# Layer 1's expert pages: answers written over their rows, a fourth single page in flight, and page work placed inside the last steps of the fused pass

## The chip, the cores and the metric

One core of a Trainium2 chip runs the whole program. The metric is the device time of one execution in microseconds (us). Before the change it is 1968.87 us, the median of three runs (1968.59 to 1971.76).

The engines named below are TensorE (PE in the profile, with PEld for its weight loads), VectorE (DVE), ScalarE (ACT), GpSimd (POOL) and SyncE (SP, whose DMA queue is SPq). Each works through its own instructions in order.

## The reference, cut to what matters

The model has two layers. Each is a graph step followed by a mixture of experts. The change touches the end of layer 1's graph step and its mixture:

```python
# x: 128 graphs of 64 nodes, 256 wide = 8192 rows
h = layer_norm(x, ln_gamma, ln_beta)                       # layer 1, graph step
agg = einsum('bij,bjh->bih', adj, h)
conv = einsum('bkh,ho->bko', agg, W_rel) + b_rel + einsum('bkh,ho->bko', h, W_root)
x = x + relu(conv)

xf = layernorm(x).reshape(-1, 256)                         # layer 1, experts
topk_vals, topk_idx = top_k(xf @ Wg + bg + bias, 2)        # 2 of 8 experts for a row
combine = (one_hot(topk_idx, 8) * softmax(topk_vals)[..., None]).sum(axis=1)
h = relu(einsum('td,edh->teh', xf, W1) + b1)               # 256 -> 512
y = einsum('teh,ehd->ted', h, W2) + b2                     # 512 -> 256
x = x + einsum('ted,te->td', y, combine)
```

## The kernel before

**The fused pass.** The pass that ends layer 0 and does layer 1's graph step works through 32 blocks (NB) of 256 rows. Every block goes through a list of stages, each with a lag. The helper `staggered` walks through steps; in step s a stage of lag L works on block s - L, in the order of the list. That order is the order of the instructions on TensorE, VectorE and ScalarE, since these three are scheduled by hand. So the last blocks end in steps 31 to 35, in which more and more stages have no block left.

The stages that matter here, by their functions: `output` (the chain A: residual, statistics, `hn` and `s`), `flip_h` (transposes `hn` on TensorE; ScalarE scales it to `hT`), `neighbours` (products `pz`, copied to `z`), `convolve_a` and `convolve_b` (products `pc`), `residual` (the chain R: x3, its store to the output, `xs`), `flip3` and `gate1` (transposes of `xs`, gate products `pg`), `choice` (the chain H: top two experts, marks `r1hot`), `count1` (counting products `pos`), `slots` (the chain S: the row of each token in its expert's list, `r1row`), and `place1` and `send1`, which send the rows (`xs`) to their experts' lists in a table in HBM (`r1x`) with indirect DMAs from GpSimd, four for a block.

**Pages.** An expert's list is worked off in pages of 256 rows, each with the expert's weights `pw` (W1 and b1) and the bias row `pb2`. W2 stays resident in `fw2`. A page goes through: fetch (`fetch1` asks for the rows `px` and, through `load1`, for `pw` and `pb2`, all from SyncE's queue), `flip1` (transposes to `pxT`), `up` (products `ph`, Relu on ScalarE into `phid`), `down` (products `py`), `share` (the weight p of each row, from the difference of two logits that a row carries in its last column), and `answer`. `answer` adds the bias to `py` into a tile `py_s` (three buffers), multiplies both halves by p, and adds each half to the output with an accumulating indirect DMA from GpSimd (L436), which reads `py_s` and, for the row numbers, column 256 of `px`. The adds of one page wait for those of the page before.

**The first four pages.** The pages numbered -4 to -1 belong to experts 0 to 3. They are known to be full well before the pass ends, so they need not wait for the last rows to be routed. Pages -4, -3 and -2 borrow PSUM banks of the fused pass (`places_of`: the pools `ps`, `po`, and `pz` or `pc` for the answers) and are put into its last steps by `ahead`; an entry (n, f) of `ahead`, in a stage of lag 4, runs f in step 36 + n, so that n = -4 is step 32. Page -1 and all later ones run in the loop after the pass, in which page i is fetched two positions ahead. There the pools `pt`, `ph` and `py` lie over the old banks. `px`, `pw` and `pb2` have three buffers each; `px4`, which holds the rows of a double page (two pages of one expert), has three as well.

**After the pass**, `page_lists` on VectorE (some sixty small instructions on 8 to 32 elements a partition) turns the counts into the lists of double pages, single pages and half pages (`r1tab`). SyncE reads each page's row and expert from it. The profiled execution has 28 double pages.

**Before, in the last steps:** page -4 is transposed in step 31, its up-products are done in two halves in step 32, its down-products in two halves in step 33; page -3 is transposed in step 33, and its up-products are in step 34; pages -3 and -2 are finished after the pass. Page -1's fetch is asked for after the pass, in the order W1, bias row, rows.

Of the kernel before, what the change touches and what calls it, by code (L numbers as in the profile page):

```python
# [9 lines left out]
F32 = mybir.dt.float32  # L10
# [96 lines left out]
class Router:  # L107
# [442 lines left out]
    def page_lists(self, scratch):  # L550

        v, E, n, pg = self.nc.vector, self.E, self.name, self.pg
        used = [0]

        def small(*shape):
            size = shape[0] * shape[-1] if len(shape) > 1 else shape[0]
            used[0] += size
            t = scratch[:, used[0] - size:used[0]]
            return t.rearrange("p (a b) -> p a b", b=shape[1]) if len(shape) > 1 else t

        wide = lambda t, k: t.unsqueeze(k).to_broadcast([P, 4, E])
# [12 lines left out]
        v.tensor_scalar(two, two, MAGIC, None, op0=ALU.add)  # L574
        v.tensor_scalar(two, two, -MAGIC, None, op0=ALU.add)
        v.tensor_scalar(big, left, pg / 2.0, None, op0=ALU.is_gt)
        v.scalar_tensor_tensor(half, left, 0.0, big, op0=ALU.is_gt, op1=ALU.subtract)
        v.scalar_tensor_tensor(one, two, -2.0, full, op0=ALU.mult, op1=ALU.add)
        v.tensor_add(one, one, big)
        le, at = small(4, E), small(4, E)  # L580
        exp, nth, no = (small(4) for _ in range(3))
        most = small(1)
        for m, (num, step) in enumerate(((two, 2 * pg), (one, pg), (half, 0))):
            cum = small(E)
            if m == 0:
                v.scalar_tensor_tensor(row, self.taken, float(pg), self.base, op0=ALU.mult, op1=ALU.add)
            elif m == 1:
                v.scalar_tensor_tensor(row, two, 2.0 * pg, row, op0=ALU.mult, op1=ALU.add)
            else:
                v.tensor_sub(row, self.last, left)  # L590
            v.tensor_tensor_scan(cum, num, self.zero[:, :E], 0.0, op0=ALU.add, op1=ALU.add)
            v.tensor_tensor(le, wide(cum, 1), wide(self.page, 2), op=ALU.is_le)  # L592
            v.tensor_reduce(exp, le, op=ALU.add, axis=AX.X)  # L593
            v.tensor_tensor(at, wide(self.expert, 1), wide(exp, 2), op=ALU.is_equal)  # L594
            v.tensor_mul(at, at, wide(row, 1))  # L595
            v.tensor_reduce(no, at, op=ALU.add, axis=AX.X)
            if step:
# [13 lines left out]
        v.tensor_copy(self.total_pages, most)  # L611
# [55 lines left out]
def two_layer_gnn_moe_kernel(ctx: ExitStack, tc: tile.TileContext, a: dict, out: bass.AP):  # L667
    nc = tc.nc
    x_in, adjT = a["x"], a["adjT"]
    N, D = x_in.shape  # L670
# [83 lines left out]
    W = D + 2  # L754
# [482 lines left out]
    def load1(i, e):  # L1237
        Q = pages[i]
        Q["w"] = w = wx.tile([P, F1W], F32, name="pw", bufs=3)
        nc.sync.dma_start(out=w, in_=fw1[ds(e, 1)].rearrange("o p f -> p (o f)"))  # L1240
        Q["b2"] = b2 = wx.tile([P, D], F32, name="pb2", bufs=3)
        nc.sync.dma_start(out=b2, in_=a["L1_ffn_b2"][ds(e, 1), :].to_broadcast([P, D]))

    def fetch1(i):
# [5 lines left out]
        if what == 0:  # L1250
            Q["x4"] = wx.tile([P, 4, W], F32, name="px4", bufs=3)
            Q["x"] = Q["x4"][:, :2, :]
        else:
            Q["x"] = wx.tile([P, 2, W], F32, name="px", bufs=3)
        if i < 0:
            if i == -FIRST:
                regs["first"] = r1.load_first(0, ENG.SP)
# [17 lines left out]
        Q["xT"] = xT = wx.tile([P, KD, PG], F32, name="pxT")  # L1275
        nc.scalar.copy(xT[:, :, :n * P], pt[:, :, :n * P])

    def up(i, lo=0, hi=KF):
        Q = pages[i]
        w, m = Q["w"], Q["n"] * P  # L1280
        if lo == 0:
            Q["hid"] = wx.tile([P, KF, PG], F32, name="phid")
        hid = Q["hid"]
        for c0 in range(lo, hi, Q["group"]):
            group = range(c0, c0 + Q["group"])
            ph = [Q["ph"](c) for c in group]
            for c in group:
                for k in range(KD):
                    nc.tensor.matmul(ph[c - c0][:, :m], lhsT=w[:, k * F1 + c * P:k * F1 + (c + 1) * P],  # L1289
                                     rhs=Q["xT"][:, k, :m], start=(k == 0), stop=(k == KD - 1))  # L1290
            for c in group:
                nc.scalar.activation(hid[:, c, :m], ph[c - c0][:, :m], AF.Relu,  # L1292
                                     bias=w[:, KD * F1 + c:KD * F1 + c + 1], scale=1.0)

    def down(i, e, tiles=(0, 1)):
        Q = pages[i]
# [17 lines left out]
        nc.vector.tensor_scalar(p, p, 1.0, None, op0=ALU.add)  # L1314
        nc.vector.reciprocal(p, p)

    def answer(i):
        Q = pages[i]
        y, p, n = wx.tile([P, 2, D], F32, name="py_s", bufs=3), Q["p"], Q["n"]
        nc.vector.tensor_add(y[:, :n, :], Q["py"][:, :n, :], Q["b2"].unsqueeze(1).to_broadcast([P, n, D]))  # L1320
        for t in range(n):
            nc.vector.tensor_scalar(y[:, t, :], y[:, t, :], p[:, t:t + 1], None, op0=ALU.mult)  # L1322
            r1.add(i // 2 * 2 if 0 <= i < 2 * ND else i, Q["x"][:, t, :], y[:, t, :])

    with tc.tile_pool(name="c3", bufs=1, reuse_waits="tile") as c3, \
            tc.tile_pool(name="work3", bufs=2, reuse_waits="tile") as work, \
# [238 lines left out]

        for i in (-4, -3, -2):
            places_of(i)

        staggered(NB, (
            (-2, load3),  # L1570
            (-3, load_weights),
            (-4, load_y),
            (2, R),
            (0, A),
            (2, R),
# [14 lines left out]
            (2, R),  # L1590
            (0, A),
            (-2, mixture),
            (1, flip_h),
            (4, ahead((-4, lambda: up(-4, 0, 2)))),
            (2, R),
            (-1, out_proj),
            (3, H),
# [17 lines left out]
            (4, lambda b: send1(b, 3) if b < NB - 2 else None),  # L1615
            (1, convolve_a),
            (3, count1),
            (4, ahead((-3, lambda: down(-4, 0, (0,))), (-2, lambda: up(-3)))),
            (-3, fold),
            (0, A),  # L1620
            (3, S),
# [2 lines left out]
            (0, A),  # L1624
            (3, S),
            (2, flip3),
            (4, ahead((-5, lambda: flip1(-4)), (-3, lambda: flip1(-3)))),
            (1, convolve_b),
            (2, gate1),
            (4, ahead((-8, lambda: fetch1(-4)), (-7, lambda: fetch1(-3)), (-6, lambda: fetch1(-2)),  # L1630
                      (-4, lambda: up(-4, 2)), (-3, lambda: down(-4, 0, (1,))))),
            (0, A),
            (3, S),
            (3, S),
            (3, S),
            (3, place1),
            (4, load_w2),
        ))
        r1.page_lists(work.tile([P, 512], F32, name="scratch", bufs=1))
        share(-4)  # L1640
        answer(-4)
        flip1(-2)
        down(-3, 1)
        up(-2)
        share(-3)
        answer(-3)


    with tc.tile_pool(name="pt4", bufs=2, space=PSUM, reuse_waits="tile") as pt_pool, \
# [7 lines left out]
        def finish(i):  # L1657
            if i >= 0:
                what, m, new = listed(i)
                if i < E1:  # L1660
                    r1.fill_end(i)
                if new and not (what == 0 and i % 2):
                    regs["e", what] = r1.load(what + 1, m, ENG.PE)
            share(i)
            down(i, regs["e", what][m % 4] if i >= 0 else i + FIRST)
            answer(i)

        def then(f):
            return lambda i: f(i) if i > -2 else None

        def fetch(i):
            places_in(i)
            if i > -2:
                fetch1(i)

        def run(order):
# [47 lines left out]
```

## Time and profile before

| | |
|---|---|
| median of three runs | 1968.87 us |
| the profiled execution | 1970.99 us |
| its span, first to last instruction | 1969.2 us |
| TensorE busy | 1852.8 us (94%) |
| VectorE busy | 1146.4 us (58%) |
| ScalarE busy | 1002.0 us (51%) |
| GpSimd busy | 1134.5 us (58%) |
| mean granted TensorE clock | 0.973 |
| fused pass ends, page loop begins | about 1475 us |
| last instruction | about 1958 us |

The profile is of one execution. A page of it sums busy time by engine and by group of instructions; the chain of waits is followed back from the last instruction, at each step to what released it. The timeline lists instructions in order of time: start, duration, engine, line, operation, output and inputs, and in brackets how long the engine stood idle before it and what ended that. In the table of windows each row has, for a stretch of time, the busy time and number of instructions of TensorE, its weight loads, VectorE, ScalarE and GpSimd, then PEclk (the granted TensorE clock as a share of full speed), the share of the DMA engines in use, and GB/s. A line of waits gives who waited for whom, the total in us, how often, and the longest.

### The profile page before, as it was taken

Reading aid. Unit: us, or ns where it says so; the run is one execution under the profiler, and the core shown is the slowest. Engines: PE = TensorE matmul, PEld = TensorE weight load, DVE = VectorE, ACT = ScalarE, POOL = GpSimd, SP = SyncE. Lnnn points to the kernel's source line nnn. Section 1 sums busy time; section 2 is a strip of 40 time slices with the busy share of each in tenths; the row PEclk is TensorE's granted clock in tenths of the full one; section 3 lists DMA queues with packets and bytes.
Section 4 is the critical chain, followed back from the end, with each engine's and each line's share of the span. In section 5 each row is a group of like instructions: output and inputs, shape, how many; then the busy total and the mean of one; then the engine's idle time right before and its main releaser. Section 6 shows DMA issues by size and latency. Waiting matters only on the chain. (4 is left out here: it accounts for less than half of the span.)

```text
span 1969.2 us, 35306 instructions
## 1 busy us (share of the span) xinstructions
PE 1852.8 (94%) x9906; PEld 1613.4 (82%) x9906; DVE 1146.4 (58%) x4256; ACT 1002.0 (51%) x2047; POOL 1134.5 (58%) x1114
## 2 busy tenths in 40 slices
PE   7999999999966899999999899999987999999996
PEld 6888888888845777888877788888876888888885
DVE  5899999999975333344433379999962222222221
ACT  5888888988841222222222266666642333333332
POOL 1377777777677677777777724444443444434443
PEclk9999999999967999999999899999988999999998
DMA  5134555553376988766666799778425666666653
GB/s 139 63 131 143 164 162 163 159 165 131 118 258 216 301 257 264 213 213 206 207 208 191 295 307 337 272 258 281 155 88 129 161 133 130 131 134 130 129 108 48
DMA packets 253085, 359.49 MB, mean 183 GB/s; under 512 B 53176, under 2 KB 210504, under 8 KB 252880
## 3 DMA queue, kind: packets, MB, share of 16 engines
q1 hardware_dynamic: 175904, 210.74, 36.0%
q0 software_dynamic: 62736, 135.21, 23.2%
q10 hardware_dynamic: 14240, 11.12, 1.8%
q8 instruction: 90, 1.47, 0.3%
q14 instruction: 115, 0.94, 0.2%
HBM read 193.27 MB, written 166.03 MB: 182 GB/s over the span
## 5 line engine op out<-in xcount | busy, mean ns | idle before, releaser
L419 POOL DMA_INDIRECT r0x<-xs,r0row x384 | 388.0, 1010 | 216.2 <-ACT lat L883 113.6
L426 POOL DMA_INDIRECT r0y<-px x390 | 378.7, 971 | 122.9 <-DMA r0y<-px 52.2
L1188 PE MATMUL py<-lat,pxT 128*128 x1616 | 385.6, 383 | 21.0 <-ACT pxT L1162 17.7
L436 POOL DMA_INDIRECT out_x<-py_s,px x131 | 202.8, 1548 | 282.5 <-DVE py_s L1322 179.3
L1192 DVE TENSOR_SCALAR px<-py,px 128x256 f32<-128x256 f32 x390 | 171.0, 480 | 306.9 <-PE py L1188 300.7
L1188 PEld LDWEIGHTS py<-lat,pxT 128*128 128x128 f32 x1616 | 293.1, 191 | 60.3 <-ACT pxT L1162 22.2
L1162 ACT COPY pxT<-pt 128x512 f32<-128x512 f32 x188 | 109.7, 586 | 345.3 <-PE pt L1159 241.0
L1292 ACT ACTIVATE phid<-ph,pw 128x256 f32<-128x256 f32 (+1 forms) x264 | 122.0, 462 | 293.0 <-PE ph L1289 180.4
L419 POOL DMA_INDIRECT r1x<-xs,r1row x128 | 134.9, 1054 | 184.1 <-ACT hn L1432 53.9
L894 PE MATMUL ps<-lat 128*128 128x256 f32 x1024 | 240.0, 383 | 0.0
L858 PE MATMUL ph<-lat 128*128 128x256 f32 x1024 | 233.3, 387 | 2.7 <-DVE lat L881 2.0
L1303 PE MATMUL py<-fw,phid 128*128 (+1 forms) x1016 | 232.7, 382 | 0.0
L1289 PE MATMUL ph<-pxT,pw 128*128 128x256 f32 (+1 forms) x1056 | 227.0, 368 | 0.0
L858 PEld LDWEIGHTS ph<-lat 128*128 128x128 f32 x1024 | 195.9, 194 | 29.8 <-issue 2.4
L894 PEld LDWEIGHTS ps<-lat 128*128 128x128 f32 x1024 | 194.3, 192 | 28.3
L1289 PEld LDWEIGHTS ph<-pxT,pw 128*128 128x128 f32 x1056 | 193.0, 190 | 24.7
L1303 PEld LDWEIGHTS py<-fw,phid 128*128 128x128 f32 x1016 | 189.6, 192 | 23.5
L1314 DVE TENSOR_SCALAR p<-p 128x2 f32<-128x2 f32 (+1 forms) x69 | 12.2, 177 | 218.5 <-ACT p L1313 218.5
L1159 PE MATMUL pt<-ident,px 128*128 128x128 f32 x780 | 120.7, 276 | 11.6 <-DMA px<-r0x 11.6
L1320 DVE TENSOR_TENSOR py_s<-py,pb 128x512 f32<-128x512 f32 (+1 forms) x67 | 44.5, 664 | 143.7 <-PE py L1303 141.4
L1159 PEld LDWEIGHTS pt<-ident,px 128*128 128x128 f32 x780 | 97.3, 142 | 36.1 <-issue 10.9
L881 DVE SCALAR_TENSOR_TENSOR lat<-ph,c_L_gnn_b,rms 128x256 f32<-128x256 f32 x256 | 111.9, 476 | 23.0 <-ACT rms L72 22.9
(337 smaller groups left out, 2966.9 us busy)
## 6 DMA issues: line engine op xcount, KB each, us to landing
y<-r0y SPq DMA_DIRECT2D x64, 768.0 KB
px<-r0x SPq DMA_DIRECT2D x376, 129.0 KB
pw<-in_L_ffn_W1b SPq DMA_DIRECT2D x41, 514.0 KB
x<-x SPq DMA_DIRECT2D x64, 256.0 KB
px<-r1x SPq DMA_DIRECT2D x28, 516.0 KB
r0x<-r0filler ACTq DMA_DIRECT2D x64, 129.0 KB
lat<-in_x SPq DMA_DIRECT2D x32, 256.0 KB
lat<-in_L_ffn_lattice_weights SPq DMA_DIRECT2D x8, 1024.0 KB
```

Source lines behind the costliest of these rows:

```text
L419: i = self.nc.gpsimd.indirect_dma_start(out=self.table[:, :], out_offset=bass.IndirectOffsetOnAxis(ap=row[:, t, k:k + 1], axis=0), in_=xs[ ...
L426: d = self.nc.gpsimd.indirect_dma_start(out=self.answer[:, :], out_offset=bass.IndirectOffsetOnAxis(ap=x[:, self.D:self.D + 1].bitcast(I32 ...
L436: i, d = f"{self.name}add{i}", self.nc.gpsimd.indirect_dma_start(out=self.total[:, :], out_offset=bass.IndirectOffsetOnAxis(ap=x[:, self.D ...
L858: nc.tensor.matmul(ph[:, c, :], lhsT=w1[:, k, ts(2 * j + c, P)], rhs=B["aggT"][:, k, :], start=(k == 0), stop=(k == KD - 1))
L881: nc.vector.scalar_tensor_tensor(hT[:, c, :], B["ph", c // 2][:, c % 2, :], b1[:, c:c + 1], B["rms"], op0=ALU.add, op1=ALU.mult)
L894: nc.tensor.matmul(B["po"][:, t, :], lhsT=B["hT"][:, c, ts(t, P)], rhs=w2[:, c, :], start=False, stop=(t == T - 1 and c == KH - 1))
L1159: nc.tensor.transpose(pt[:, k, ts(q, P)], Q["px"][:, q, ts(k, P)], ident)
L1188: nc.tensor.matmul(py[:, q, :], lhsT=xT[q][:, k, ts(h, P)] if parts == 2 else xT[:, k, ts(q, P)], rhs=lat[:, ds(e, 1), k, :].rearrange("p ...
L1192: nc.vector.tensor_scalar(px[:, q, :D], py[:, q, :], px[:, q, D + 1:D + 2], None, op0=ALU.mult)
L1289: nc.tensor.matmul(ph[c - c0][:, :m], lhsT=w[:, k * F1 + c * P:k * F1 + (c + 1) * P], rhs=Q["xT"][:, k, :m], start=(k == 0), stop=(k == KD ...
L1292: nc.scalar.activation(hid[:, c, :m], ph[c - c0][:, :m], AF.Relu, bias=w[:, KD * F1 + c:KD * F1 + c + 1], scale=1.0)
L1303: nc.tensor.matmul(py[:, t, :], lhsT=Q["hid"][:, c, ts(t, P)], rhs=fw2[:, ds(e, 1), c, :].rearrange("p o d -> p (o d)"), start=(c == 0), s ...
```

## The change

It has four parts.

- `answer` is split into `gather` (the bias add), `weight` (the two multiplications) and `add1` (the two adds). The result is written into the first 256 columns of the page's own rows, and `py_s` is gone.
- `px` and `pb2` have four buffers in place of three. Page -1 is fetched in step 32 of the list (its rows and bias row are requested as early as SyncE's queue allows; its weights take page -4's buffer), and not in the loop.
- `up` is split into `products` (TensorE) and `bend` (the Relus on ScalarE), for two of the four column groups at a time, and these are spread over steps 31 to 33. The transposes of pages -4, -3 and -2 move to steps 30, 31 and 33; page -4's down-products, both halves, come between the gate products of step 32 and the counts of step 33; page -4's bias add is at the end of step 33. After the pass page -2's up-products come first, and then page -3's down-products.
- For blocks 30 and 31 `flip_h` stands at the head of the step, and not in its middle. In `page_lists` four small instructions that the list of double pages doesn't need are moved behind that list.

```diff
@@ page_lists
-        v.tensor_scalar(big, left, pg / 2.0, None, op0=ALU.is_gt)
-        v.scalar_tensor_tensor(half, left, 0.0, big, op0=ALU.is_gt, op1=ALU.subtract)
-        v.scalar_tensor_tensor(one, two, -2.0, full, op0=ALU.mult, op1=ALU.add)
-        v.tensor_add(one, one, big)
...
             elif m == 1:
+                v.tensor_scalar(big, left, pg / 2.0, None, op0=ALU.is_gt)
+                v.scalar_tensor_tensor(half, left, 0.0, big, op0=ALU.is_gt, op1=ALU.subtract)
+                v.scalar_tensor_tensor(one, two, -2.0, full, op0=ALU.mult, op1=ALU.add)
+                v.tensor_add(one, one, big)
@@ load1, fetch1
-        Q["b2"] = b2 = wx.tile([P, D], F32, name="pb2", bufs=3)
+        Q["b2"] = b2 = wx.tile([P, D], F32, name="pb2", bufs=4)
...
-            Q["x"] = wx.tile([P, 2, W], F32, name="px", bufs=3)
+            Q["x"] = wx.tile([P, 2, W], F32, name="px", bufs=4)
@@ up becomes products and bend
+    def products(i, c0):
+        Q = pages[i]
+        m = Q["n"] * P
+        for c in range(c0, c0 + Q["group"]):
+            Q["up", c] = Q["ph"](c)
+        for c in range(c0, c0 + Q["group"]):
+            for k in range(KD):
+                nc.tensor.matmul(Q["up", c][:, :m], lhsT=Q["w"][:, k * F1 + c * P:k * F1 + (c + 1) * P],
+                                 rhs=Q["xT"][:, k, :m], start=(k == 0), stop=(k == KD - 1))
+
+    def bend(i, c0):
...
+        for c in range(c0, c0 + Q["group"]):
+            nc.scalar.activation(Q["hid"][:, c, :m], Q["up", c][:, :m], AF.Relu,
+                                 bias=Q["w"][:, KD * F1 + c:KD * F1 + c + 1], scale=1.0)
+
+    def up(i):
+        for c in range(0, KF, pages[i]["group"]):
+            products(i, c)
+            bend(i, c)
@@ answer becomes gather, weight and add1
-        y, p, n = wx.tile([P, 2, D], F32, name="py_s", bufs=3), Q["p"], Q["n"]
-        nc.vector.tensor_add(y[:, :n, :], Q["py"][:, :n, :], Q["b2"].unsqueeze(1).to_broadcast([P, n, D]))
-        for t in range(n):
-            nc.vector.tensor_scalar(y[:, t, :], y[:, t, :], p[:, t:t + 1], None, op0=ALU.mult)
-            r1.add(i // 2 * 2 if 0 <= i < 2 * ND else i, Q["x"][:, t, :], y[:, t, :])
+        y, n = Q["x"], Q["n"]
+        nc.vector.tensor_add(y[:, :n, :D], Q["py"][:, :n, :], Q["b2"].unsqueeze(1).to_broadcast([P, n, D]))
...
+            nc.vector.tensor_scalar(y[:, t, :D], y[:, t, :D], p[:, t:t + 1], None, op0=ALU.mult)
...
+            r1.add(i // 2 * 2 if 0 <= i < 2 * ND else i, Q["x"][:, t, :], Q["x"][:, t, :D])
@@ the list of stages
+        usual = NB - 2
...
+            (1, lambda b: flip_h(b) if b >= usual else None),
             (2, R),
...
-            (1, flip_h),
-            (4, ahead((-4, lambda: up(-4, 0, 2)))),
+            (1, lambda b: flip_h(b) if b < usual else None),
+            (4, ahead((-5, lambda: products(-4, 0)), (-5, lambda: bend(-4, 0)),
+                      (-4, lambda: bend(-4, 2)), (-4, lambda: products(-3, 0)), (-3, lambda: down(-4, 0, (1,))))),
...
-            (4, ahead((-3, lambda: down(-4, 0, (0,))), (-2, lambda: up(-3)))),
+            (4, ahead((-4, lambda: bend(-3, 0)))),
...
-            (4, ahead((-5, lambda: flip1(-4)), (-3, lambda: flip1(-3)))),
+            (4, ahead((-6, lambda: flip1(-4)), (-5, lambda: flip1(-3)), (-3, lambda: flip1(-2)))),
             (1, convolve_b),
             (2, gate1),
             (4, ahead((-8, lambda: fetch1(-4)), (-7, lambda: fetch1(-3)), (-6, lambda: fetch1(-2)),
-                      (-4, lambda: up(-4, 2)), (-3, lambda: down(-4, 0, (1,))))),
+                      (-4, lambda: fetch1(-1)), (-5, lambda: products(-4, 2)), (-4, lambda: down(-4, 0, (0,))),
+                      (-3, lambda: products(-3, 2)))),
...
             (3, place1),
             (4, load_w2),
+            (4, ahead((-3, lambda: bend(-3, 2)), (-3, lambda: gather(-4)))),
         ))
         r1.page_lists(work.tile([P, 512], F32, name="scratch", bufs=1))
-        share(-4)
-        answer(-4)
-        flip1(-2)
+        up(-2)
         down(-3, 1)
-        up(-2)
-        share(-3)
-        answer(-3)
+        for i in (-4, -3):
+            share(i)
+            if i == -3:
+                gather(i)
+            weight(i)
+            add1(i)
@@ the page loop
-            answer(i)
+            gather(i)
+            weight(i)
+            add1(i)
...
-            if i > -2:
+            if i >= 0:
                 fetch1(i)
```

More of the change, by code (lines that the diff above doesn't have):

```diff
@@ L1276, in flip1 @@
         nc.scalar.copy(xT[:, :, :n * P], pt[:, :, :n * P])
-    def up(i, lo=0, hi=KF):
+    def products(i, c0):
         Q = pages[i]
-        w, m = Q["w"], Q["n"] * P
-        if lo == 0:
-            Q["hid"] = wx.tile([P, KF, PG], F32, name="phid")
[L1283 to L1293, printed above, removed]
+        m = Q["n"] * P
[7 more added lines that the diff above has]
+        Q = pages[i]
+        m = Q["n"] * P
+        if c0 == 0:
+            Q["hid"] = wx.tile([P, KF, PG], F32, name="phid")
+        for c in range(c0, c0 + Q["group"]):
[5 more added lines that the diff above has]
+            bend(i, c)
     def down(i, e, tiles=(0, 1)):
@@ L1315, in share, with gather, weight, add1 @@
         nc.vector.reciprocal(p, p)
-    def answer(i):
+    def gather(i):
         Q = pages[i]
-        y, p, n = wx.tile([P, 2, D], F32, name="py_s", bufs=3), Q["p"], Q["n"]
-        nc.vector.tensor_add(y[:, :n, :], Q["py"][:, :n, :], Q["b2"].unsqueeze(1).to_broadcast([P, n, D]))
-        for t in range(n):
-            nc.vector.tensor_scalar(y[:, t, :], y[:, t, :], p[:, t:t + 1], None, op0=ALU.mult)
-            r1.add(i // 2 * 2 if 0 <= i < 2 * ND else i, Q["x"][:, t, :], y[:, t, :])
+        y, n = Q["x"], Q["n"]
+        nc.vector.tensor_add(y[:, :n, :D], Q["py"][:, :n, :], Q["b2"].unsqueeze(1).to_broadcast([P, n, D]))
+    def weight(i):
+        Q = pages[i]
+        y, p, n = Q["x"], Q["p"], Q["n"]
+        for t in range(n):
+            nc.vector.tensor_scalar(y[:, t, :D], y[:, t, :D], p[:, t:t + 1], None, op0=ALU.mult)
+    def add1(i):
+        Q = pages[i]
+        for t in range(Q["n"]):
+            r1.add(i // 2 * 2 if 0 <= i < 2 * ND else i, Q["x"][:, t, :], Q["x"][:, t, :D])
     with tc.tile_pool(name="c3", bufs=1, reuse_waits="tile") as c3, \
```

## The prediction

> **What bounds the kernel now.** I read the chain of work that ended last, then TensorE's timeline around the chain's only large break, then the queue of SyncE (SPq). From 1487 us to the end the chain is TensorE alone (up-products L1289, down-products L1303, transposes L89), 7.35 us a page, so whatever brings the start of that steady run forward is gained in full. The chain in order of time:
>
> ```profile
> 1478.76 1.62 POOL out_x L436
> 1480.68 3.71 DMA out_x<-py_s,px
> 1484.59 2.63 DMA px<-r1x
> 1487.26 1.11 PE pt L89 x4
> 1488.38 5.71 PE py L1303 x16
> 1494.09 3.45 PE ph L1289 x16
> 1497.54 0.44 PE pt L89 x4
> 1497.98 3.46 PE py L1303 x16
> ```
>
> Page -1's rows (`px`) may be fetched only once page -4's answers have been added to the output: three `px` buffers for four pages. The transpose at 1497.54 is that of the first double page; it is my mark for "the run is steady". TensorE's timeline shows this wait and two small ones before it:
>
> ```profile
> 1432.62 0.63 PE L89 MATMUL ps<-ident,hn 128*128 128x128 f32 x4
> 1435.91 3.78 PE L1460 MATMUL pz<-m_rel,hT 128*128 128x256 f32 x8 [2.65 <-ACT hT L1452]
> ...
> 1457.97 0.20 PE L269 MATMUL pos<-r1hot,r0tri 128*128 128x16 bf16 x2 [2.41 <-DVE r1hot L254]
> ...
> 1465.57 0.20 PE L269 MATMUL pos<-r1hot,r0tri 128*128 128x16 bf16 x2
> ...
> 1487.26 1.11 PE L89 MATMUL pt<-ident,px 128*128 128x128 f32 x4 [10.55 <-DMA px<-r1x]
> ```
>
> In the table of windows, read PEclk (before the last two columns):
>
> ```profile
> 1436.00:1440.00 4.00, 4.00 (x10) 3.01 (x11) 3.06 (x18) 1.94 (x4) 1.90 (x3) 0.50 0.09 33
> 1460.00:1464.00 4.00, 3.76 (x20) 3.15 (x20) 0.06 (x1) 1.07 (x2) 3.09 (x4) 0.74 0.33 115
> 1488.00:1492.00 4.00, 4.00 (x11) 3.20 (x10) 0.34 (x2) 0.69 (x2) 0.63 (x1) 0.50 0.96 306
> ```
>
> Each wait is followed by a slow stretch: 8 products that take 1.89 us on the timeline took 3.78 at 1435.91, the 16 of L1303 at 1488 took 5.71 instead of 3.46. In SyncE's waits, what held its queue at the end:
>
> ```profile
> SPq L1242 <- DVE py_s L1322: 21.6, 1, 21.6
> SPq L644 <- DMA out_x<-py_s,px: 5.8, 1, 5.8
> ```
>
> Page -1's bias row (L1242, a fourth request for three `pb2` buffers) stood at the head for 21.6 us, and behind it page -1's rows and all the double pages.
>
> [...]gaps of 1.5 to 1.8 us around 770 and 793 us left PEclk at 1.00, so a short stall costs its own length. [...]page -1's 258 KB took 2.63 us here[...]. [...]here the wait for page -4's add took 3.71 us, and this chain of page adds stays.
>
> **The change part by part.** The parts move the same 16-product groups (1.73 us for 8, 3.46 for 16), so I lay the new order on the old durations, from 1430.8 us on. Pages -4 to -1 are the four single ones; blocks 30 and 31 the last of the pass.
>
> Step 30: page -4's transpose (0.44) now comes here, and its copy (0.59 busy, 0.48 apart) delays `hn` of block 30 on ScalarE. The gate products end at 1433.06, not 1432.62, and `hn` is ready at about 1433.1.
>
> Step 31: block 30's transposes (0.44) now head the step, and so does hT on ScalarE, whose 2.65 us wait came from standing behind two square roots that wait for VectorE. Beside hT (done about 1435.1) TensorE does page -4's first products, 1433.5 to 1435.3. Then pz 1.73, bias and pc 1.95, counts 0.1, xs 0.44, page -3's transpose 0.44, z 0.87, gate 0.9, page -4's second products 1.73: 1443.5. The moved square roots make VectorE late by some 0.1 us; nothing waits for that.
>
> Step 32: hn 0.44, page -3's first products 1.73, pz 1.73, pc 1.95, counts 0.1, xs 0.44, z 0.87, gate 0.9, page -4's down-products 3.46: 11.6 us, to 1455.1. Block 30's marks (r1hot) are ready at about 1454.2: pc's end 1450.8 plus the 3.4 us that the residual, its statistics, two ScalarE steps and the choice take in the trace of before. So 3.46 us of page work lies over the 2.41 us wait.
>
> Step 33: counts 0.1, xs 0.44, page -2's transpose 0.44, 0.2 for its neighbour's copy, gate 0.9, page -3's second products 1.73: 1458.9. Block 31's marks: gate end 1457.2 plus 1.2 plus about 0.2 for the inserted bias add of page -4 (0.67, mostly in idle VectorE time): 1458.6, just in time. Block 31's counts start at X = 1459.0; before, 1465.57. That is 6.6 us, and it moves the whole routing chain with it: sends, page table, first double fetch. Eight Relus moved on ScalarE (0.47 each) lie in its idle time (25 of 68 us busy from 1432 to 1500).
>
> After X, TensorE: pages -2 up 3.46, -3 down 3.46, -1 transposed 0.44, -2 down 3.46, and the first quarter of -1 up 0.87: X+11.8, with no wait for rows, because page -1's rows, bias and weights came steps earlier (weights follow page -4's last Relu, about 1446). The 10.55 us wait and the 2.8 us of slow clock behind it (0.67 + 2.25) go. What is late next: the second quarter uses the bank that held page -3's answers, and waits for VectorE's bias add of page -3, which stands behind the page table. VectorE from the same counts: 1.56 us to the table's start (1465.57 to 1467.13), 10.1 us of table (to 1477.23), 0.28 + 0.63 for page -4's shares and weights, 0.15 and 0.67 for page -3's: X+13.4. TensorE stalls 1.6 us there; before, this wait was hidden in the long one. Then 2.6 us of products: the double page is transposed at X+16.0 = 1475.0.
>
> Are its rows there? Block 31's four sends follow block 30's on GpSimd (1.27 us apart): last issued about 1466.5, landed 2.1 us later (3.71 less 1.6 of issue) at 1468.6. The table's first part, shorter by the four instructions that were moved down (0.6 us), is done at 1465. The 516 KB fetch starts about 1468.8: [...]4.2 as the packets of its counterpart behind another fetch took: 1472 to 1473. The W1 page behind it is needed only at 1478. Cover of 2 us or more.
>
> Adds: page -4's starts at 1471.5 and each page's pair waits for the one before, 6.5 us (1478.76 to 1485.23), so the first double's adds start near 1497.7, some 4 us late, and land by 1507; the fourth double, which takes its buffer, is transposed at 1519. A group of four adds takes 4 x 1.85 + 2.9 = 10.3 us, less than a double's 14.7, so the backlog drains. Answers written over the rows free no engine time: the same add (0.69) and multiplications (0.35), and the `px` buffer was held by the row numbers anyway. I cost that at nothing, since VectorE stands idle before each page.
>
> Sum: 1497.5 - 1475.0 = 22.5 us. The profiled execution took 1970.99 us around a span of 1969.2; it becomes 1948.5. The median of before is 1968.87, 2.1 below; so **1946.4 us**.
>
> **Rivals.** (1) The routing chain isn't moved: the waits are filled, but X stays near 1465.6, because marks depend on VectorE and ScalarE, not on TensorE's place. For it: both small waits name those engines. Against: hT's wait came only from order, and VectorE itself waited 1.7 to 3.5 us for counts. Then VectorE's X+13.4 decides, the mark is at 1481.6, the gain 15.9 us: 1953.0. (2) The fetch of the first double takes the place of page -1's: sends crowd, or it shares the DMA engines with W1 pages (busy 0.95 at 1488 to 1500). It needs over 2 us; with 4 us more and a slow stretch, 1949 to 1953. (3) No stall at the page -3 bank, a TensorE dense throughout: 1.6 us better, 1944.8. (4) Slower: accumulating DMAs out of 1032-byte-pitched rows cost more than out of `py_s`. GpSimd has 14.7 us for a double and uses 10.3; beyond 14.7 the adds set the pace for 28 doubles, and from 15.5 on the 22.5 us are lost. At 16 us a double: 28 x 1.3 - 22.5 = 14 us slower, 1983. Against: layer 0's replies leave pitched `px` rows at 0.97 us each.
>
> **How the numbers follow.** Forecast 0.66 (its own range 1944.5 to 1949), dense 0.08, no moved chain 0.10, late fetch 0.11, slower 0.03, no gain 0.02. Below 1944 TensorE would have to do less work; 1954 takes in rivals 1 and 2. A measurement tells 0.2% (4 us) from no change. Faster 0.95, same 0.02, slower 0.03.
>
> **What would show it.** Right: no wait for `px<-r1x` between the last counts and the first double; pz of block 30 without a wait; one TensorE wait of 1 to 2 us on `px<-pc`; PEclk 1.00 from 1436 to 1476; the first `px4` transpose near 1475. Wrong: that transpose waiting for a DMA, last counts later than 1461, or GpSimd waiting for `out_x` adds past 1520.

## The result and the profile after

The changed kernel takes 1949.02 us, the median of five runs (1948.74 to 1952.36); five runs of the kernel before, the first three among them, have the median 1968.87 us (1967.98 to 1971.76). The ratio is 0.9901, with a 95% interval of 0.9889 to 0.9912: about 20 us faster. The profiled execution took 1948.88 us around a span of 1947.1 us; before, it was 1970.99 around 1969.2. In two of the four sittings below (sets of runs taken together; the two are e1 to e4 and e5 to e8) every kernel, the one before included, took some 320 us longer, all but a few of them ahead of step 30 of the pass; so runs are compared by intervals inside their traces, and by ratios to the kernel before of the same sitting.

The chain of waits of the kernel after, around the place where the kernel before had its break (start, duration, what):

```profile
1472.54 2.86 PE ph L1285 x12
1475.40 0.44 PE pt L89 x4
1475.83 3.46 PE py L1310 x16
```

The second line is the first double page, the mark of the prediction: 1475.40, where the kernel before had 1497.54. That is 22.1 us, and the spans differ by 22.1 us as well: everything after the mark takes as long as before. TensorE's timeline of the kernel after shows how the stretch before it was closed:

```profile
1433.22 1.89 PE L1285 MATMUL ps<-pxT,pw 128*128 128x256 f32 x8
1434.95 1.89 PE L1475 MATMUL pz<-m_rel,hT 128*128 128x256 f32 x8
...
1451.34 3.70 PE L1310 MATMUL pz<-fw,phid 128*128 128x256 f32 x16
1454.87 0.20 PE L269 MATMUL pos<-r1hot,r0tri 128*128 128x16 bf16 x2
...
1459.06 0.20 PE L269 MATMUL pos<-r1hot,r0tri 128*128 128x16 bf16 x2
...
1466.16 0.60 PE L89 MATMUL pt<-ident,px 128*128 128x128 f32 x4
...
1472.54 2.86 PE L1285 MATMUL ph<-pxT,pw 128*128 128x256 f32 x12 [1.46 <-DVE px L1327]
1475.23 0.60 PE L89 MATMUL pt<-ident,px 128*128 128x128 f32 x4
```

Page work (L1285, L1310) stands directly ahead of `pz` and of the counts `pos`, and neither carries a bracket any more: no idle time ahead of them. Block 31's counts are at 1459.06 and were at 1465.57. Page -1's rows are there when TensorE comes to them (1466.16, no bracket). One wait of more than 0.3 us is left, 1.46 us on the PSUM bank of page -3's answers. The windows of the kernel after (columns as before, PEclk before the last two):

```profile
1436.00:1440.00 4.00, 4.00 (x27) 3.46 (x27) 3.50 (x23) 2.89 (x7) 2.00 (x3) 1.00 0.09 33
1460.00:1464.00 4.00, 4.00 (x21) 3.51 (x19) 3.48 (x26) 2.02 (x6) 3.08 (x4) 1.00 0.33 118
1472.00:1476.00 4.00, 3.46 (x18) 3.08 (x19) 2.89 (x8) 1.73 (x5) 2.84 (x2) 1.00 0.95 233
1488.00:1492.00 4.00, 4.00 (x22) 3.54 (x21) 0.35 (x3) 2.28 (x6) 2.29 (x2) 1.00 0.18 13
```

PEclk is 1.00 where it was 0.50, 0.74 and 0.50, and stays there through the 1.46 us wait in the third row. What still holds SyncE's queue at the end of the pass:

```profile
SPq L624 <- DVE scratch L584: 13.7, 1, 13.7
...
SPq L652 <- DMA r1x<-xs,r1row: 3.2, 1, 3.2
```

The 21.6 us behind page -1's bias row are gone. The queue waits for the page table (L624), and then 3.2 us more for the last rows to be sent (L652): the sends, not the table, set when the first double is fetched.

### The profile page after: what moved, and what is told of

It is laid out like the page before. It is cut to its first block, busy times and chain, and to the rows that moved or that the text cites. A ratio compares the mean times of both kernels' runs of the same rounds, so it can differ in the third digit from the quotient of the medians.

```text
span 1947.1 us, 35284 instructions
## 1 busy us (share of the span) xinstructions
PE 1845.0 (95%) x9906; PEld 1608.8 (83%) x9906; DVE 1146.9 (59%) x4256; ACT 1001.6 (51%) x2047; POOL 1134.5 (58%) x1114
## 5 line engine op out<-in xcount | busy, mean ns | idle before, releaser
L436 POOL DMA_INDIRECT out_x<-px x131 | 202.8, 1548 | 265.9 <-DVE px L1333 173.7
L1310 PE MATMUL py<-fw,phid 128*128 (+1 forms) x1016 | 230.4, 380 | 0.0
L1285 PE MATMUL ph<-pxT,pw 128*128 128x256 f32 (+1 forms) x1056 | 227.3, 368 | 1.5 <-DVE px L1327 1.5
L1285 PEld LDWEIGHTS ph<-pxT,pw 128*128 128x128 f32 x1056 | 193.2, 190 | 26.3 <-DVE px L1327 1.9
L1310 PEld LDWEIGHTS py<-fw,phid 128*128 128x128 f32 x1016 | 188.2, 190 | 22.5
L1327 DVE TENSOR_TENSOR px<-py,pb 128x512 f32<-128x512 f32 (+1 forms) x67 | 44.5, 664 | 138.3 <-PE py L1310 133.7
```

The lines of the kernel that those rows point to most:

```text
L436: i, d = f"{self.name}add{i}", self.nc.gpsimd.indirect_dma_start(out=self.total[:, :], out_offset=bass.IndirectOffsetOnAxis(ap=x[:, self.D ...
L1285: nc.tensor.matmul(Q["up", c][:, :m], lhsT=Q["w"][:, k * F1 + c * P:k * F1 + (c + 1) * P], rhs=Q["xT"][:, k, :m], start=(k == 0), stop=(k ...
L1310: nc.tensor.matmul(py[:, t, :], lhsT=Q["hid"][:, c, ts(t, P)], rhs=fw2[:, ds(e, 1), c, :].rearrange("p o d -> p (o d)"), start=(c == 0), s ...
```

## The experiments

A common measure: from the first counting product of step 30 to block 31's counts, to the first double page's transpose, and to the end of the span, all in us from each run's trace. (The span of the kernel before ends at 1969.2 us; about 1958, given above for its last instruction, is where its last add to the output ends on GpSimd.)

| run | block 31's counts | first double | end of the span | ratio to before (95%) |
|---|---|---|---|---|
| before, first trace | 35.33 | 67.14 | 538.96 | |
| e9_before | 35.33 | 67.53 | 539.48 | |
| after, first trace | 29.16 | 45.33 | 517.20 | 0.9901 (0.9889 to 0.9912) |
| e1_buffers | 35.32 | 53.65 | 525.42 | 0.9930 (0.9904 to 0.9956) |
| e2_three_buffers | 29.93 | 62.63 | 534.35 | 0.9972 (0.9942 to 1.0001) |
| e12_three_buffers | 29.17 | 59.80 | 531.65 | 0.9971 (0.9962 to 0.9980) |
| e3_inplace | 35.27 | 67.59 | 539.39 | 0.9993 (0.9970 to 1.0017) |
| e4_gather_in_table | 30.00 | 44.55 | 517.07 | 0.9897 (0.9850 to 0.9944) |
| e5_control | 29.20 | 51.19 | 523.39 | 0.9917 (0.9877 to 0.9958) |
| e6_gather_in_table | 29.93 | 44.38 | 516.90 | 0.9835 (0.9771 to 0.9900) |
| e7_flip_late | 30.43 | 51.42 | 523.44 | 0.9925 (0.9898 to 0.9952) |
| e8_gather_first | 29.92 | 48.28 | 524.39 | 0.9909 (0.9870 to 0.9947) |
| e10_lists_old | 29.17 | 45.23 | 516.95 | 0.9891 (0.9874 to 0.9907) |
| e11_gather_in_table | 29.17 | 43.61 | 515.53 | 0.9887 (0.9870 to 0.9903) |

**The fourth page's buffers alone.**

```diff
@@ the kernel before
-        Q["b2"] = b2 = wx.tile([P, D], F32, name="pb2", bufs=3)
+        Q["b2"] = b2 = wx.tile([P, D], F32, name="pb2", bufs=4)
...
-            Q["x"] = wx.tile([P, 2, W], F32, name="px", bufs=3)
+            Q["x"] = wx.tile([P, 2, W], F32, name="px", bufs=4)
...
-        y, p, n = wx.tile([P, 2, D], F32, name="py_s", bufs=3), Q["p"], Q["n"]
+        y, p, n = Q["x"], Q["p"], Q["n"]
...
-                      (-4, lambda: up(-4, 2)), (-3, lambda: down(-4, 0, (1,))))),
+                      (-4, lambda: fetch1(-1)), (-4, lambda: up(-4, 2)), (-3, lambda: down(-4, 0, (1,))))),
...
-            if i > -2:
+            if i >= 0:
                 fetch1(i)
```

> The kernel before with nothing but the room for a fourth single page: four px and pb2 buffers, answers written over their rows (py_s gone), page -1 fetched in step 32; the order of TensorE's work is as before. Theory (two gains side by side: the wait for page -1's rows, and the routing chain that starts 6.6 us earlier): block 31's counts stay at 1465.6, the 10.55 us wait and the slow clock behind it go, the first double page is transposed at 1484 to 1485.5 (1476.56 plus 0.44 + 3.46 + 3.46, a bank wait of 0 to 1.5 us), against 1497.4: 12 to 13.4 us faster, 1955.5 to 1957. Rival A (the fourth buffer is the whole gain): the mark near 1475, 1947. Rival B (another wait takes the place of this one, the double's rows or page -4's add): the mark after 1490, under 7 us faster.

TensorE's timeline of e1_buffers:

```profile
1783.66 0.19 PE L269 MATMUL pos<-r1hot,r0tri 128*128 128x16 bf16 x2 [2.41 <-DVE r1hot L254]
...
1791.30 0.20 PE L269 MATMUL pos<-r1hot,r0tri 128*128 128x16 bf16 x2
...
1802.29 0.60 PE L89 MATMUL pt<-ident,px 128*128 128x128 f32 x4
1802.72 3.62 PE L1303 MATMUL py<-fw,phid 128*128 128x256 f32 x16
1806.18 3.62 PE L1289 MATMUL ph<-pxT,pw 128*128 128x256 f32 x16
1809.63 0.60 PE L89 MATMUL pt<-ident,px 128*128 128x128 f32 x4
```

The two small waits of the last steps stay (the 2.41 us one is shown), the counts are where they were (35.32), and from them on TensorE runs without a wait. The first double comes 13.5 to 13.9 us earlier than in the two traces of the kernel before. The expectation's 1484 to 1485.5 is 53.8 to 55.3 in this measure, so the mark came at its early end, with no bank wait: here page -3's bias add is done before its bank is asked for. Both rivals fall.

**Everything but these buffers**, in two sittings:

```diff
@@ the changed kernel
-        Q["b2"] = b2 = wx.tile([P, D], F32, name="pb2", bufs=4)
+        Q["b2"] = b2 = wx.tile([P, D], F32, name="pb2", bufs=3)
...
-            Q["x"] = wx.tile([P, 2, W], F32, name="px", bufs=4)
+            Q["x"] = wx.tile([P, 2, W], F32, name="px", bufs=3)
...
-                      (-4, lambda: fetch1(-1)), (-5, lambda: products(-4, 2)), (-4, lambda: down(-4, 0, (0,))),
+                      (-5, lambda: products(-4, 2)), (-4, lambda: down(-4, 0, (0,))),
...
-            if i >= 0:
+            if i > -2:
                 fetch1(i)
```

> The changed kernel with three px and pb2 buffers and page -1 fetched in the loop again; page work over the waits, flip_h early and the page table as changed. Theory: block 31's counts stay at 1459.1; page -1's rows wait for page -4's add, which lands near 1477, so TensorE waits some 14 us for px and runs on a slow clock after it; first double transposed at 1490 to 1491 (the counts plus the 32 us of the kernel before): 6.5 to 7.2 us faster than before, about 1962. With e1_buffers' 12 to 13.4 that makes less than the whole 22.2, so each part is worth more with the other. Rival (page work over the waits gains nothing, since the marks depend on VectorE and ScalarE): counts at 1465.6, the time of before, 1969. Rival (the buffers are not what held page -1): 1949.

> The version of e2_three_buffers, where VectorE paused 0.7 us before block 31's marks and 1.5 us after its counts. Without these pauses, theory: counts of block 31 29.2 us after those of step 30, and the first double page at 60.4 us (62.6 less 2.2), 6.7 to 7.1 us earlier than in the kernel before; ratio 0.9965. The two parts of the change alone then give 13.5 to 13.9 and about 7 us, and together 21.8 to 22.3: little over one us is owed to having both. Rival (the pauses were part of its price): 62.6 again, 4.5 to 4.9 us.

TensorE's timeline of e12_three_buffers, and then its windows:

```profile
1461.22 0.20 PE L269 MATMUL pos<-r1hot,r0tri 128*128 128x16 bf16 x2
...
1482.46 1.09 PE L89 MATMUL pt<-ident,px 128*128 128x128 f32 x4 [13.98 <-DMA px<-r1x]
1483.34 5.22 PE L1310 MATMUL py<-fw,phid 128*128 128x256 f32 x16
1488.40 3.62 PE L1285 MATMUL ph<-pxT,pw 128*128 128x256 f32 x16
1491.85 0.60 PE L89 MATMUL pt<-ident,px 128*128 128x128 f32 x4
```

```profile
1484.00:1486.00 2.00, 2.00 (x6) 1.55 (x6) 0.34 (x2) 0.28 (x2) 0.00 (x0) 0.50 1.13 330
1486.00:1488.00 2.00, 2.00 (x10) 1.73 (x9) 0.00 (x0) 0.00 (x0) 0.00 (x0) 0.85 0.67 158
```

The counts come as early as in the changed kernel (29.17), but TensorE only waits longer for page -1's rows, 13.98 us, with the slow clock behind it (0.50, 0.85). The first double is 7.3 to 7.7 us earlier than before, a little more than the 6.7 to 7.1 expected; the times give 5.8 us, with an interval (3.9 to 7.5 us of 1970) that just takes it in. In e2 the same wait was 15.78 us, behind pauses of VectorE that also put the counts 0.8 us later; e12, without these pauses, shows that they were no part of the price (its rival falls). With the row above: 13.5 to 13.9 for the buffers, 7.3 to 7.7 for the order of the work, and 21.8 to 22.3 for both. The two gains nearly add: set against one and the same trace of the kernel before, 0.6 to 1.1 us are owed to having both.

**Answers written over their rows, alone:**

```diff
@@ the kernel before
-        y, p, n = wx.tile([P, 2, D], F32, name="py_s", bufs=3), Q["p"], Q["n"]
+        y, p, n = Q["x"], Q["p"], Q["n"]
```

> The kernel before with only the answers written over their rows, three buffers as before. Theory: no change, 1968.9 within 1.5 us, the bias add and multiplications 0.67 and 0.35 us as before, and the wait of 10.55 us for px stays within 0.5. Rival (accumulating DMAs out of rows 1032 bytes apart cost more than out of py_s): up to 16 us a double, 1983; any size shows in the spacing of GpSimd's adds.

Ratio 0.9993 (0.9970 to 1.0017), first double at 67.59 against 67.53 in e9_before; its wait for page -1's rows is 11.73 us (10.81 in e9_before), so the "within 0.5" of 10.55 is missed while the sum holds. In the traces nothing is gained and nothing lost; the times alone, from 7 us faster to 4 us slower of 2297, would not tell so finely. The groups with shapes kept apart say the same, the kernel before first and then the one after (the number after the bar is busy time, then mean ns):

```profile
L436 POOL DMA_INDIRECT out_x<-py_s,px x131 | 202.8, 1548 | 282.5 <-DVE py_s L1322 179.3 <-issue 47.4 <-DMA out_x<-py_s,px 37.5
L1322 DVE TENSOR_SCALAR py_s<-py_s,p 128x256 f32<-128x256 f32 x131 | 41.2, 354 | 2.4
```

```profile
L436 POOL DMA_INDIRECT out_x<-px x131 | 202.8, 1548 | 265.9 <-DVE px L1333 173.7 <-DMA out_x<-px 52.6 <-issue 32.7
L1333 DVE TENSOR_SCALAR px<-px,p 128x256 f32<-128x256 f32 x131 | 41.8, 359 | 2.4
```

What it buys is room: three `py_s` tiles hold 6 KB a partition (3 x 512 numbers), and the fourth `px` and `pb2` take 3 KB of it (516 and 256 numbers). Whether these would have fitted beside `py_s` was not tried.

**The last wait, 1.46 us.** Page -3's bias add is put between the second and the third list of the page table:

```diff
@@ the changed kernel
-    def page_lists(self, scratch):
+    def page_lists(self, scratch, between):
...
             else:
+                between()
                 v.tensor_sub(row, self.last, left)
...
-        r1.page_lists(work.tile([P, 512], F32, name="scratch", bufs=1))
         up(-2)
         down(-3, 1)
+        r1.page_lists(work.tile([P, 512], F32, name="scratch", bufs=1), lambda: gather(-3))
         for i in (-4, -3):
             share(i)
-            if i == -3:
-                gather(i)
             weight(i)
```

> The changed kernel with the bias add of page -3 put between the second and the third list of the page table on VectorE, where TensorE has just finished that page's products. Theory: the wait of 1.46 us on its bank goes, the first double is transposed at 1473.8 in place of 1475.2, its rows being there by 1473; the third list ends 0.7 us later, for which nothing waits: 1.4 us faster than the changed kernel, 1947.6. Rival (the first double's rows are late): TensorE waits for px<-r1x instead and the gain is 0 to 0.8 us. Rival (the later weights of page -4 push its adds, and the chain of adds decides): no faster than 1949, with a wait for out_x at a later double.

> The changed kernel itself, as the mark for the runs beside it. From the counts of step 30 (the pos product that precedes block 30's transposes) to the first double page's transpose it took 45.3 us in its first trace, against 67.1 in the kernel before; the same is expected here within 0.3, with the 1.46 us wait on the bank of page -3's answers.

> As e4_gather_in_table, beside the changed kernel on one chip. Theory: 1.4 us faster than e5_control, 43.9 us from the counts of step 30 to the first double page, no wait on the bank. Rival (the first double's rows come next): a wait of TensorE for px<-r1x takes part of it.

> The version of e6_gather_in_table in more rounds, as the one that may beat both kernels. Theory: 44.4 us from the counts of step 30 to the first double as in e4 and e6 (43.8 where VectorE pauses nowhere), no wait on the bank, and a ratio to the kernel before of 22.2 + 1.4 us or better: 0.9880 at 1969 us, 0.9897 at 2290 us, below that where the changed kernel's own table is paused as in e5_control. Rival (the bank wait was an accident of e5_control's chip, and is worth nothing elsewhere): the changed kernel's ratio, 0.9901 to 0.9917.

The timeline of VectorE in e11, and then that of TensorE (its lines stand one further down than in the changed kernel):

```profile
1470.05 0.15 DVE L610 SCALAR_TENSOR_TENSOR scratch<-scratch 128x1 f32<-128x1 f32 x1
1470.12 0.68 DVE L1328 TENSOR_TENSOR px<-pc,pb 128x512 f32<-128x512 f32 x1
1470.72 0.16 DVE L591 TENSOR_TENSOR scratch<-r1last,scratch 128x8 f32<-128x8 int32 x1
```

```profile
1471.63 3.62 PE L1286 MATMUL ph<-pxT,pw 128*128 128x256 f32 x16
1475.08 0.60 PE L89 MATMUL pt<-ident,px 128*128 128x128 f32 x4
```

All sixteen up-products of page -1 now run in one piece; in the kernel after they were four, the wait, and twelve. The first double comes 1.6 to 1.7 us earlier (43.61 against 45.23 and 45.33) with its rows there, and the end of the span 1.4 to 1.7 us earlier. The later adds of page -4 show no effect. In e4 and e6 VectorE paused ahead of block 31's counts, which came 0.8 us later than in the kernel after. From these counts to the first double they gain as much as e11 (14.6 and 14.5 us, and 16.2 in the kernel after), but at the end of the span only 0.1 to 0.3 us are left. This version, as e11 ran it, is the fastest of the traces, 23.4 to 24.0 us ahead of the kernel before. The times agree (1950.18 us against 1951.58 of e10, which differs from the changed kernel by four small instructions, and 1972.80 before) but don't separate it: the intervals of the ratios overlap.

e5_control missed its expectation. VectorE's timeline in it, inside the table, and TensorE's behind it:

```profile
1785.97 0.16 DVE L601 SCALAR_TENSOR_TENSOR scratch<-scratch 128x4 f32<-128x4 f32 x1 [1.02 <-issue]
```

```profile
1788.03 2.86 PE L1310 MATMUL py<-fw,phid 128*128 128x256 f32 x12 [1.57 <-ACT phid L1294]
1794.62 5.49 PE L1285 MATMUL ph<-pxT,pw 128*128 128x256 f32 x12 [2.87 <-DVE px L1327]
```

Pauses, some with nothing to wait for ("issue"), made the table 12.4 us long (1780.21 to 1792.62; 9.9 us in the first trace, 1460.63 to 1470.54). With ScalarE's own 1.57 us ahead of it, the bank wait grew from 1.46 to 2.87 us, and this time the clock was slow behind it (PEclk 0.73 from 1792 to 1796, 0.50 from 1796 to 1800): the twelve products took 5.49 us, not 2.86. The second list of the table ended at 1790.69; a bias add placed there would have been done at 1791.4, before TensorE came to the bank at 1791.75 (1794.62 less 2.87). That it would have saved both the wait and the slow products is worked out and not shown: e4 and e6, at 44.55 and 44.38, had no such pauses inside the table.

**How much cover the first double's rows have.**

```diff
@@ the changed kernel
-        r1.page_lists(work.tile([P, 512], F32, name="scratch", bufs=1))
         up(-2)
         down(-3, 1)
+        gather(-3)
+        r1.page_lists(work.tile([P, 512], F32, name="scratch", bufs=1))
```

The bias add of page -3 further down is taken out in return.

> The changed kernel with the bias add of page -3 ahead of the whole page table on VectorE, which then waits for that page's products and starts the table some 6 us later. Theory (the first double's rows have about 2 us of cover): the fetch is asked for some 3 us later[...]; TensorE waits 2 to 3 us for px<-r1x in place of the 1.46 on the bank: first double 0.5 to 2 us later than in e5_control, and a slow stretch after the wait may add up to 3. Rival (the sends, not the table, set the fetch, so the table has room to spare): 1.4 us earlier than e5_control, as e6.

SyncE's timeline in e8, and then TensorE's:

```profile
1806.03 0.39 SPq L652 DMA_DIRECT2D px<-r1x  x1
```

```profile
1809.79 1.12 PE L89 MATMUL pt<-ident,px 128*128 128x128 f32 x4 [3.76 <-DMA px<-r1x]
1812.56 5.49 PE L1310 MATMUL py<-fw,phid 128*128 128x256 f32 x16 [1.65 <-ACT phid L1294]
```

The fetch is asked for at 1806.03 and used at 1809.79, the first moment at which TensorE can: 3.76 us. The 4.2 us that the prediction gave these 516 KB are 0.4 us more. In the kernel after the request is at 1468.98, so the rows were there near 1472.7 and were needed at 1475.23: 2.5 us of cover. Delayed past it, TensorE waits and then runs slowly (the sixteen products at 1812.56 took 5.49 us, the sixteen at 1798.95, ahead of the wait, 3.62), and the span ends 1.0 us later than in e5_control, which has its own wait, and 7.2 us later than in the first trace after. The first double itself missed its expectation: it comes 2.9 us earlier than in e5_control, not 0.5 to 2 later, because e5_control's mark is late by its own paused table; against the first trace after it is 2.95 us later. TensorE's wait was 3.76 us where 2 to 3 were expected. The rival (room to spare) falls.

**flip_h late, and the page table's order as before:**

```diff
@@ e7_flip_late
-        usual = NB - 2
+        usual = NB
@@ e10_lists_old
+        v.tensor_scalar(big, left, pg / 2.0, None, op0=ALU.is_gt)
...
         for m, (num, step) in enumerate(((two, 2 * pg), (one, pg), (half, 0))):
...
-                v.tensor_scalar(big, left, pg / 2.0, None, op0=ALU.is_gt)
```

Of the four instructions only the first is shown.

> The changed kernel with flip_h of blocks 30 and 31 back in the middle of the step. Theory: hT of block 30 stands behind two square roots again and comes 2.65 us after its transposes; page -4's first products (1.73 us) lie in that wait, so pz waits 0.7 to 1.0 us, too short to slow the clock; counts of block 31 and first double 0.7 to 1.0 us later than in e5_control. Rival (page work hides it whole, the early flip_h is worth nothing): 0.0. Rival (the wait is back in full, with its slow clock of 1.9 us): 3 to 4.5 us later.

> The kernel before itself, as the mark for e1_buffers to e3_inplace on a chip like theirs. In its first trace the counts of block 31 came 35.3 us and the first double page 67.1 us after the counts of step 30. Theory: 35.3 again (the order there is set by TensorE), and 67.1 to 68.5, since page -1's rows came up to 1.2 us later in e3_inplace and the table ran 2.4 us longer in e5_control.

> The changed kernel with the four small instructions of the page table back ahead of the list of double pages. Theory: nothing in the total: the double list is ready 0.6 us later, but the fetch of the first double waits 1.9 to 3.2 us for the sends after it, and the table as a whole is no longer or shorter; the first double within 0.3 us of the changed kernel's (45.3 us after the counts of step 30) where VectorE runs the table in 10 us. Rival: the fetch moves with the list, and the double with it, 0.6 us later.

TensorE's timeline in e7:

```profile
1751.09 1.89 PE L1285 MATMUL ps<-pxT,pw 128*128 128x256 f32 x8
1753.87 2.02 PE L1475 MATMUL pz<-m_rel,hT 128*128 128x256 f32 x8 [0.89 <-ACT hT L1467]
```

Page -4's products cover most of the wait for hT, 0.89 us are left, the eight products behind it take 2.02 us (3.78 behind the 2.65 us wait of the kernel before), and block 31's counts come 1.23 us later than in e5_control, a little more than the 0.7 to 1.0 expected. At these counts the early flip_h is worth about a microsecond. What it is worth in the time isn't shown: the first double (51.42) can't be set against e5_control's (51.19), since VectorE paused in both, in e5_control inside the table and in e7 for 2.4 us ahead of it, and the ratios overlap. e9_before fits its expectation in both intervals. The four moved instructions gain nothing at the mark: 45.23 us with them in the old place, 45.33 without; in e10 the fetch still waits 2.7 us for the sends, after the list is ready.

## Why the prediction was right, step by step

The mark was forecast at 1475.0 and came at 1475.4; the gain 22.5 us, and it was 22.1; the profiled execution 1948.5 us, and it was 1948.88. The forecast of the median, 1946.4, is 2.6 us below 1949.02 although the steps are right. The term that was mis-sized is the last one of the sum, "2.1 below": the profiled execution of the kernel before had been 2.1 us above its median, and this was subtracted from the new one. The profiled execution after was 0.14 us below its median. The 2.1 was the luck of one execution (the five runs before spread over 3.8 us) and nothing that the change carries over. In a later sitting the medians fell by 21.2 us (e10) where here they fell by 19.9 (17.3 to 21.9 by the ratio's interval). So 1949.02 lies at the upper end of the range given for the forecast (1944.5 to 1949), and at the lower end of what rival 2 allowed (1949 to 1953). The number alone would not have chosen between the two; the trace does, in which the first double waits for no rows.

- Steps 30 to 33: block 31's counts were forecast at 1459.0 and stand at 1459.06. Page -4's down-products end at 1455.0 (forecast 1455.1), and block 30's marks are ready at 1453.9 (1454.2), so the wait is covered by 1 us. That the routing chain moves with them, which rival 1 denied, is shown by 29.16 against 35.33 and by e12, where it moves without the buffers.
- From the counts to the mark: 16.2 us (forecast 16.0). The new wait, forecast at 1.6 us on page -3's bank, was 1.46. Its cause is the bias add behind the page table, as e11 shows by moving it; what rival 3 gave for a dense TensorE, 1.6 us, is what e11 gains at the mark.
- The first double's rows: last send forecast at 1466.5, seen at 1466.12; fetch forecast at 1468.8, seen at 1468.98; cover 2 us or more (the "or more" rested on no trace), 2.5 by e8's fetch. Rival 2 was close, but didn't happen.
- Answers in place at no cost: e3 and the two groups above. Rival 4 is gone.
- Page adds every 6.5 us: wrong in size, without consequence. GpSimd's timeline of the kernel after, and of e12_three_buffers:

```profile
1471.63 1.62 POOL L436 DMA_INDIRECT out_x<-px  x1 [4.53 <-DVE px L1333]
1473.56 1.58 POOL L436 DMA_INDIRECT out_x<-px  x1 [0.30 <-DVE p L1322]
1482.54 1.55 POOL L436 DMA_INDIRECT out_x<-px  x1 [7.40 <-DMA out_x<-px]
...
1503.72 1.55 POOL L436 DMA_INDIRECT out_x<-px  x1 [3.62 <-DMA out_x<-px]
```

```profile
1473.84 1.62 POOL L436 DMA_INDIRECT out_x<-px  x1 [4.61 <-DVE px L1333]
1475.76 1.58 POOL L436 DMA_INDIRECT out_x<-px  x1 [0.30 <-issue]
1480.30 1.55 POOL L436 DMA_INDIRECT out_x<-px  x1 [2.96 <-DMA out_x<-px]
```

From page -4's adds to page -3's it took 10.9 us, not 6.5; with three buffers, where no page is fetched beside page -4's add, it took 6.46, and the next pair there, beside fetches, followed after 11.0 (at 1491.30). In the kernel after the double pages' rows and weights are fetched in the same microseconds (a DMA share of 0.95 from 1472 to 1476). That these are what slows the adds is what the two orders suggest; it was not tried by itself. The first double's adds start at 1503.72, 6 us later than forecast, and that used up most of the room: the fourth double, which takes the first one's buffer, has its rows asked for at 1513.33 and is transposed at 1519.31. That is 6.0 us, where the forecast left 12, and 2.2 us more than the fetch in e8 took. The backlog drains: from 1546 to 1600 GpSimd waits for VectorE before each page and no longer for the adds, and TensorE has no idle time from the mark to the end. One sign that was to show the prediction wrong, GpSimd waiting for adds past 1520, came by the letter and tells nothing: there are nine such waits after 1600, and seven past 1520 in the kernel before, and TensorE stands idle in neither.

- The clock: that a short stall costs its own length came true for the new wait, whose 1.46 us passed at PEclk 1.00; moving it away gained 1.4 to 1.7 us at the end of the span (e11). The waits that the prediction went by, at 768 and 793 us of the kernel before, were 1.77 and 1.81 us, also at 1.00. At what length of a wait the clock falls was not shown (last section).

## What to carry to other kernels

Where one engine is the bound, take the last few steps before its steady run, list its waits, and lay there the work that it will have to do later anyway; a wait filled ahead of a chain of small dependent steps also moves that chain. Ask of every wait that is removed which one was hidden behind it, here a bank released by one addition in the wrong place of VectorE's queue, and how far the next is from deciding. Compare a profile with a profile and a median with a median: the distance between the two is noise, and isn't carried over.

## What the runs showed of the hardware

In the last steps of these runs the granted clock fell at waits of 2.41 and 2.65 us (the kernel before: PEclk 0.50 from 1459 to 1462 and from 1435 to 1441) and of 2.87 us (e5_control: 0.50 from 1796 to 1800). It stayed at 1.00 through the wait of 1.46 us (the kernel after, 1472 to 1476) and that of 1.57 us (e5_control, 1788 to 1792); behind the one of 0.89 us (e7_flip_late) the eight products took 2.02 us. By length alone the waits don't sort, though. The kernel after (first line) and e12_three_buffers (second) have these waits earlier in the program, and the eight products behind the shorter one, 2.00 us, are the slow ones (2.74 us, against 1.99 behind 3.34):

```profile
793.92 2.74 PE L1188 MATMUL py<-lat,pxT 128*128 x8 [2.00 <-ACT pxT L1162]
```

```profile
665.52 1.99 PE L1188 MATMUL py<-lat,pxT 128*128 x8 [3.34 <-ACT pxT L1162]
```

In the kernel after PEclk was 0.50 from 796 to 798 us, behind the first of these waits. What else decides was not shown.

What a wait cost went with the clock: 1.46 us of waiting at the whole clock cost 1.4 to 1.7 us by e11, and 2.87 us of waiting came with twelve products that took 2.63 us more (5.49 less 2.86).
